# A gated recurrent layer on one Trainium2 core: its input products computed by a seven-product matrix algorithm nested twice, over 16 steps at a time

## The chip, the cores and the metric

The kernel runs on one core of one Trainium2 chip. The metric is the device time of one execution in microseconds. The profile is that of one execution, taken by the hardware profiler; PE is TensorE's matmuls, PEld its weight loads, DVE is VectorE, ACT ScalarE, POOL GpSimd, SP SyncE.

## The reference

B = 8 sequences, T = 512 steps, 512 inputs, 512 hidden units, all float32.

```python
def step(h, x_t):
    fused = jax.nn.sigmoid(jnp.concatenate([x_t, h], axis=-1) @ w_W + w_b)
    hidden_state, output_state = jnp.split(fused, 2, axis=-1)
    memory_state = x_t @ wx_W + wx_b + hidden_state * (h @ wh_W + wh_b)
    h_new = output_state * h + (1.0 - output_state) * jnp.tanh(memory_state)
    return (h_new, h_new)
_, hs = jax.lax.scan(step, h0, xT)
x = x + jnp.swapaxes(hs, 0, 1)
```

The products with x_t do not depend on h and can be computed steps ahead (the x side). The products with h are the recurrence: each step needs the one before.

## The kernel before, in words

**Layout.** The 512 units are four chunks k of 128 partitions. A matmul has a stationary operand of 128 x 32 (for h: 32 columns, in which the 8 sequences of a step have their place; for x: 4 steps x 8 sequences) and writes 32 of the 128 PSUM partitions; j = 0 to 3 selects which. Four matmuls with j = 0 to 3 run side by side in the array (a quad). A float32 matmul is issued as two instructions (passes). hT holds the state, in two halves: hTA (chunks 0 and 1) and hTB (chunks 2 and 3), in rings of NH = 8 steps.

**One step i** (line 370). TensorE first runs the recurrent matmuls in the order of ORDER: A0 A1 (256 columns, from hTA), A2 A3 (192, from hTB), D0 to D3 (128), H2 H3 (64), all accumulating on a bank that already holds the x side's part. Behind them `take(later, 1)` (line 397) issues one portion of x-side matmuls, up to the next `yield` in `products`. TensorE runs in this program order, so the x portion of step i lies between H of step i and A of step i + 1. On VectorE and ScalarE follows the chain of the step: `turn_r` transposes A's result (tr, line 415), ScalarE takes the sigmoid (md0A, line 226), VectorE scans (m, line 403), ScalarE takes tanh, and `update(0, q)` scans the new hTA (line 403), on which A0 and A1 of the next step wait. The same for the second half ends in `update(1, q)`, hTB, on which A2 and A3 wait. Behind these scans VectorE has the x-side work of the step, and two fillers (line 593); the next thing on it is tr of the next step. GpSimd adds x to the new state (ot, lines 594 to 600 and 615), behind hTB. The transpose of line 430 waits for the add of seven steps earlier.

**The x side.** Four steps are a group g; chunks c of 16 steps (four groups) are loaded by SP (`load_x`, three chunks ahead) and stored by SP (`store`). Groups 0 to 3 are computed plainly (`prefill`, 16 matmuls of 384 columns, four per yield). From there on, a block o of 8 steps (two groups) goes through `products` (line 296): the product of a 2 x 2 block matrix of x (2 groups of steps by 2 halves of the inputs) with a 2 x 2 block matrix of wx (2 halves of the inputs by 2 halves of the outputs) by seven block products instead of eight. The block sums of wx (tw) are made once on VectorE (`weight_sum`), those of x (sx) on GpSimd (`x_sum`), and the sums of the products are partly accumulated in the PSUM tiles xps and partly made by VectorE and ScalarE when these are read (lines 530 to 584). The results are in xs, one tile of 576 columns for each of two groups. ScalarE's `spread` (line 256) copies xs of the next group into the banks A, D and H, and `turn_x` (line 262) transposes its part X into md1 on VectorE, one piece a step.

What orders all this is the program order on each engine; the schedule is written by hand (lines 523 to 591: o is the block, u the step within it).

Of the kernel before, what the change touches and what calls it, by code (L numbers as in the profile page):

```python
# [13 lines left out]
P = 128  # L14
NQ = 4
# [19 lines left out]
WIDE = 384  # L35

SUMS = ((2,), (2,), (2, 1), (2, 1), (1,), (1, 3), (3,), (3, 3))

Q01, Q23 = slice(0, 64), slice(64, 128)
# [9 lines left out]
def tile_cond_rnn_residual(  # L49
# [100 lines left out]
    hT = [[pair(n, f"hT{n}{i}", 32, 3) for i in range(NH)] for n in "AB"]  # L150
# [22 lines left out]

    tw = [const.tile([P, 2, 2, WIDE], F32, name=f"tw{n}") for n in range(4)]
    sx = [[const.tile([P, 2, GS * B], F32, name=f"sx{n}{q}") for q in range(2)] for n in range(4)]
    step_bias = const.tile([P, HALF], F32, name="stepbias")
    xs = [const.tile([P, 576], F32, name=f"xs{n}") for n in range(2)]
    u2 = const.tile([P, WIDE], F32, name="u2")
    u3 = const.tile([P, WIDE], F32, name="u3")
    both = const.tile([P, WIDE], F32, name="both")  # L180

# [28 lines left out]
    nc.vector.tensor_copy(bias, xps[0])  # L210
    for t_ in xs:
        nc.gpsimd.memset(t_[:, :64], 0.0)
        nc.gpsimd.tensor_copy(t_[:, 64:128], bias[:, :64])
        nc.gpsimd.tensor_copy(t_[:, 512:], bias[:, 448:])
    for hf in range(2):
# [32 lines left out]
    def prefill_two():  # L248
        yield from prefill(2)
        yield from prefill(3)  # L250

    def source(g, c0, c1):

        return xs[g % 2][:, c0:c1] if g else xps[0][:, c0 - 64 : c1 - 64]
# [12 lines left out]
    def wx_of(kh, nh):  # L267
        return wx[:, 2 * kh : 2 * kh + 2, 2 * nh : 2 * nh + 2]

    def x_half(o, n, kh):  # L270

        return x_of(o // 2, slice(2 * kh, 2 * kh + 2), 8 * (o % 2) + GS * n, GS)

    def weight_sum(n, k=slice(0, 2), j=slice(0, 2)):

        a, b = [
            (wx_of(0, 1), wx_of(0, 0)),
            (wx_of(1, 1), tw[0]),
            (wx_of(1, 1), wx_of(0, 1)),
            (wx_of(1, 0), tw[1]),  # L280
        ][n]
        at = (slice(0, P), k, j)
        nc.vector.tensor_tensor(tw[n][at], a[at], b[at], ALU.subtract)  # L283

    def x_sum(o, n):

        t_ = [q[o % 2] for q in sx]
        a, b, op = [
            (x_half(o, 1, 0), x_half(o, 1, 1), ALU.add),
            (t_[0], x_half(o, 0, 0), ALU.subtract),  # L290
            (x_half(o, 0, 0), x_half(o, 1, 0), ALU.subtract),
            (x_half(o, 0, 1), t_[1], ALU.subtract),
        ][n]
        nc.gpsimd.tensor_tensor(t_[n], a, b, op)

    def products(o):

        t_ = [q[o % 2] for q in sx]
        p1 = (0, x_half(o, 0, 0), wx_of(0, 0))
        p2 = (0, x_half(o, 0, 1), wx_of(1, 0))  # L300
        p3 = (0, t_[3], wx_of(1, 1))
        p4 = (1, x_half(o, 1, 1), tw[3])
        p6 = (0, t_[1], tw[1])
        p7 = (1, t_[2], tw[2])

        def pair(left, right, k, c0=0, c1=WIDE):
            for j in range(NQ):
                bank, lhs, rhs = left if j < 2 else right
                mm(
                    xps[bank][32 * j : 32 * j + 32, COLS.start + c0 : COLS.start + c1],  # L310
                    lhs[:, k],
                    rhs[:, k, j % 2, c0:c1],
                    start=right is p7 and k == 0 and c0 == 0 and j >= 2,
                )

        def shared(k):
            for j in range(NQ):
                c0 = HALF * (1 - j // 2)
                mm(
                    xps[j // 2][32 * j : 32 * j + 32, COLS.start : COLS.start + HALF],  # L320
                    t_[0][:, k],
                    tw[0][:, k, j % 2, c0 : c0 + HALF],
                )

        pair(p1, p7, 0, 0, 128)
        if o > 2:
            yield
        pair(p1, p7, 0, 128)
        pair(p1, p7, 1, 0, 56)
        yield  # L330
        pair(p1, p7, 1, 56)
        yield
        pair(p2, p6, 0)
        yield
        pair(p2, p6, 1)
        yield
        pair(p4, p3, 0, 0, 344)
        yield
        pair(p4, p3, 0, 344)
        shared(0)  # L340
        pair(p4, p3, 1, 0, 72)
        yield
        shared(1)
        pair(p4, p3, 1, 72, 208)
        yield
        pair(p4, p3, 1, 208)
# [7 lines left out]
    def x_side():  # L354
        for o in range(2, NG // 2):
            yield from products(o)
# [5 lines left out]
    first = {1: prefill(1), 2: prefill_two()}  # L362
    weight_sum(0)
    spread(0, "HDA")
    for e in range(NQ):
        turn_x(0, e)

    pool_done = {}
    summed = []
    for i in range(T):  # L370
# [23 lines left out]
        if 1 <= i < 4:  # L394
            take(first[2], 2 if i == 3 else 3)
        else:
            take(later if i else first[1], 1)

        rows = slice(B * s, B * s + B)

# [84 lines left out]
        def update(hf, q):  # L485
            s1 = (i + 1) % GS
# [36 lines left out]
        o, u = divmod(i, 2 * GS)  # L523
        nxt, two = o + 1 < NG // 2, o + 2 < NG // 2
        if i == 0:
            nc.scalar.copy(xs[1][:, SC], xps[1][:, COLS])
            spread(1, "H")
            turn_x(1, 0)
        add_ = nc.vector.tensor_tensor
        if u == 3 and o and nxt:  # L530
            add_(xs[0][Q23, SC], xps[0][Q23, COLS], both[Q23], ALU.add)
        elif u == 7 and two:
            nc.vector.tensor_copy(xs[0][Q01, SC], xps[0][Q01, COLS])
        elif u == 0 and o and nxt:
            add_(u3[Q23], xps[1][Q23, COLS], u2[Q23], ALU.add)
        ahead = 2 * o + (1 if u < 3 else 2 if u < 7 else 3)
        if ahead < NG:
            turn_x(ahead, (u + 1) % GS)
        lo = slice(COLS.start, COLS.start + HALF)
        if u == 0:  # L540
            spread(2 * o + 1, "D")
            if o and nxt:
                nc.scalar.copy(xps[0][Q01, lo], step_bias[Q01])
                nc.scalar.copy(xps[1][Q23, lo], step_bias[Q23])
        elif u == 1:
            spread(2 * o + 1, "A")
            if o == 0:
                seed(3)
        elif u == 2:
            if o == 0:  # L550
                nc.scalar.copy(xs[0][:, SC], xps[0][:, COLS])
            elif nxt:
                nc.scalar.copy(both[Q23, HALF:], xps[0][Q01, lo])
                nc.vector.tensor_copy(both[Q23, :HALF], xps[1][Q23, lo])
            if two:
                nc.scalar.copy(xps[0][Q01, COLS], bias[Q01, COLS])
                if o:
                    x_sum(o + 2, 2)
        elif u == 3:
            if o == 0:  # L560
                nc.scalar.copy(xs[1][:, SC], xps[1][:, COLS])
                x_sum(o + 2, 2)
        elif u == 4 and nxt:
            if o:
                add_(xs[1][Q01, SC], xps[1][Q01, COLS], u3[Q23], ALU.add)
            spread(2 * o + 2, "A")
            if two:
                x_sum(o + 2, 0)
        elif u == 5 and nxt:
            if o:  # L570
                add_(xs[1][Q23, SC], u3[Q23], both[Q23], ALU.add)
            if two:
                nc.scalar.copy(xps[0][Q23, COLS], xps[0][Q01, COLS])
                x_sum(o + 2, 1)
            spread(2 * o + 2, "D")
        elif u == 6 and nxt:
            spread(2 * o + 2, "H")
            if two:
                nc.vector.memset(xps[1][Q01, COLS], 0.0)
                x_sum(o + 2, 3)  # L580
        elif u == 7 and nxt:
            if two:
                nc.scalar.copy(u2[Q23], xps[0][Q23, COLS])
            spread(2 * o + 3, "H")
        if i < len(SUMS):
            for n in SUMS[i]:
                weight_sum(n, *divmod(summed.count(n), 2))
                summed.append(n)
        if i == 4:
            for to, c_ in ((Q01, slice(256, 448)), (Q23, slice(64, 256))):  # L590
                nc.vector.tensor_tensor(step_bias[to], bias[Q23, c_], bias[Q01, c_], ALU.subtract)
# [22 lines left out]
        for hf in (1, 0):  # L614
# [79 lines left out]
```

## Time and profile before

| | |
|---|---|
| median of 3 runs | 1654.95 us (1654.7 to 1655.07) |
| the profiled execution | 1654.78 us, its span 1653.0 us |
| A start of step 1 | 20.10 us |
| A starts of steps 4, 14, 494 and 511 | 33.09, 65.65, 1592.34, 1645.85 us |
| granted TensorE clock, steps 14 to 493 | 1.00 |
| DVE busy, steps 14 to 493 | 1341.98 us, 2.80 a step |

An "A start" is the start of the first matmul A<-wa,hTA of a step; from one to the next is one step. In the timeline a row has its start, its length, engine, line, operation, tiles, shapes and the count of merged instructions, and in brackets the idle time before it with what ended it. Matmul ends are modelled and overlap the next matmuls, so TensorE's pace is read from starts.

### The profile page before, as it was taken

What the parts mean: (1) busy time and instruction counts of PE and PEld (TensorE: products, weight loads), DVE (VectorE), ACT (ScalarE), POOL (GpSimd) and SP (SyncE); (2) the same over time, 40 slices, a digit from 0 to 9 for tenths busy, and PEclk for the clock granted to TensorE, in tenths of its full rate; (3) what the DMA queues carried; (4) which work ended last, traced back from release to release, by engine and by line L of the source; (5) the groups of instructions that cost most, each with busy time, mean ns of one, the idle gap of its engine ahead of it and who ended that gap; (6) DMA issues with size and microseconds to landing.
All of it is one profiled execution on the core that took longest, in us unless ns stands there. A gap on an engine that the chain in (4) does not pass through costs nothing.

```text
span 1653.0 us, 114239 instructions
## 1 busy us (share of the span) xinstructions
PE 1640.8 (99%) x47566; PEld 1291.2 (78%) x47566; DVE 1438.5 (87%) x11237; ACT 1136.4 (69%) x5884; POOL 328.7 (20%) x1290
## 2 busy tenths in 40 slices
PE   8999999999999999999999999999999999999998
PEld 5777778777777777777877777777777777787776
DVE  6888888888888888888888888888888888888887
ACT  4667767667677676676776766767767667677665
POOL 2221121211211212112112121121121211211211
PEclk9999999999999999999999999999999999999999
DMA  4000000000000000000000000000000000000000
GB/s 181 17 5 17 17 17 17 16 5 17 17 17 17 5 17 17 17 17 4 17 17 17 17 15 7 17 18 17 17 4 18 17 17 17 4 17 11 11 11 10
DMA packets 11473, 30.41 MB, mean 18 GB/s; under 512 B 1221, under 2 KB 1733, under 8 KB 10953
## 3 DMA queue, kind: packets, MB, share of 16 engines
q1 hardware_dynamic: 10800, 22.94, 4.0%
q8 instruction: 372, 6.09, 1.5%
q14 instruction: 149, 1.21, 0.2%
q10 hardware_dynamic: 152, 0.16, 0.0%
HBM read 14.70 MB, written 8.39 MB: 14 GB/s over the span
## 4 chain that ended last, share of the span: by engine, by line
PE 97%; DVE 2%; DMA 1%; issue 0%; ACT 0%; DVEq 0%
PE A L195 47%; PE D L195 26%; PE xp L195 17%; PE H L195 7%; DMA wd<-in_wd_dram 1%; DVE m L403 0%; DVE tr L415 0%; DMA rows<-in_bias_dram 0%; DVE md1B L472 0%; DVE tw L283 0%; DVE md1A L430 0%; DVE hTA L403 0%; DVE tz L415 0%; DVE hTB L403 0%; DVE md1B L430 0%
## 5 line engine op out<-in xcount | busy, mean ns | idle before, releaser
L195 PE MATMUL A<-wa,hTA 128*32 128x256 f32 x8176 | 535.4, 379 | 2.8 <-DVE hTA L403 2.7
L195 PE MATMUL A<-wa,hTB 128*32 128x192 f32 x8176 | 427.8, 327 | 0.0
L195 PEld LDWEIGHTS A<-wa,hTA 128*32 128x32 f32 x8176 | 271.2, 122 | 167.5 <-DVE hTA L403 81.4
L595 POOL TENSOR_TENSOR ot<-xin,hTB 128x16 f32<-128x16 f32 x503 | 125.4, 249 | 1284.3 <-DVE hTB L403 1273.6
L195 PEld LDWEIGHTS A<-wa,hTB 128*32 128x32 f32 x8176 | 255.4, 123 | 133.3 <-DVE hTB L403 101.6
L195 PE MATMUL D<-wd,hTA 128*32 128x128 f32 x8192 | 317.6, 273 | 1.2 <-DMA wd<-in_wd_dram 1.2
L195 PE MATMUL D<-wd,hTB 128*32 128x128 f32 x8192 | 317.6, 273 | 0.0
L226 ACT ACTIVATE md0A<-tr 128x16 f32<-128x16 f32 x512 | 112.8, 220 | 239.4 <-DVE tr L415 224.9
L195 PE MATMUL xp<-tw,sx 128*32 128x192 f32 (+5 forms) x2480 | 276.3, 358 | 0.0
L195 PEld LDWEIGHTS D<-wd,hTA 128*32 128x32 f32 x8192 | 257.0, 122 | 22.5 <-DMA wd<-in_wd_dram 1.5
L415 DVE STREAM_TRANSPOSE tr<-A 128x64 f32<-128x64 f32 x511 | 127.7, 250 | 145.6 <-PE A L195 137.8
L195 PEld LDWEIGHTS D<-wd,hTB 128*32 128x32 f32 x8192 | 240.4, 122 | 0.1
L226 ACT ACTIVATE hTB<-m 128x8 f32<-128x8 f32 x1024 | 163.6, 208 | 90.0 <-DVE m L403 85.0
L195 PE MATMUL xp<-wx,xin 128*32 128x384 f32 (+4 forms) x1552 | 218.9, 384 | 0.0
L195 PE MATMUL H<-wa,hTB 128*32 128x64 f32 x8192 | 208.2, 219 | 0.0
L195 PEld LDWEIGHTS H<-wa,hTB 128*32 128x32 f32 x8192 | 185.6, 122 | 0.0
L226 ACT ACTIVATE hTB<-hTB 128x16 f32<-128x16 f32 x512 | 121.2, 237 | 85.0 <-DVE hTB L403 84.2
L403 DVE TENSOR_TENSOR_SCAN hTA<-hd0A,hTA 128x24 f32<-128x24 f32 x1024 | 175.9, 172 | 0.0
L403 DVE TENSOR_TENSOR_SCAN hTB<-hd0B,hTB 128x24 f32<-128x24 f32 x1024 | 154.4, 192 | 21.8
L226 ACT ACTIVATE hTA<-m 128x8 f32<-128x8 f32 x1024 | 160.7, 206 | 2.3
L403 DVE TENSOR_TENSOR_SCAN m<-md0B,md1B 128x24 f32<-128x24 f32 x1024 | 154.6, 192 | 1.3
L403 DVE TENSOR_TENSOR_SCAN m<-md0A,md1A 128x16 f32<-128x16 f32 x1024 | 141.9, 180 | 8.9
(104 smaller groups left out, 2717.1 us busy)
## 6 DMA issues: line engine op xcount, KB each, us to landing
xin<-in_x_dram SPq DMA_DIRECT2D x31, 256.0 KB, 3.2
out_dram<-ot SPq DMA_DIRECT2D x31, 256.0 KB, 2.1
wx<-in_wx_dram SPq DMA_DIRECT2D x4, 768.0 KB, 7.0
wa<-in_wa_dram SPq DMA_DIRECT2D x4, 512.0 KB, 9.7
wd<-in_wd_dram SPq DMA_DIRECT2D x1, 768.0 KB
wd<-in_wd_dram SPq DMA_DIRECT2D x1, 256.0 KB, 11.2
out_dram<-ot SPq DMA_DIRECT2D x1, 192.0 KB, 3.8
head<-in_xh_dram ACTq DMA_DIRECT2D x1, 144.0 KB, 5.0
```

The lines of the kernel that those rows point to most:

```text
L195: nc.tensor.matmul(out_, lhsT, rhs, start=start, stop=False, skip_group_check=True)
L226: inst = nc.scalar.activation(out_, in_, func, **kw).ins
L403: return nc.vector.tensor_tensor_scan(*[t_[:, :, c_].rearrange("p n c s -> p (n c s)") for t_ in (out_, d0, d1)], 0.0, ALU.mult, ALU.add,).ins
L415: inst = nc.vector.transpose(t_.rearrange("p c n -> p (c n)"), raw[n][hf]).ins
L595: return engine.tensor_tensor(ot[:, t, 2 * hf : 2 * hf + 2, :].rearrange("p c n -> p n c"), x_of(c, slice(2 * hf, 2 * hf + 2), t, 1).rearr ...
```

## The change

The seven-product algorithm is applied to blocks of 16 steps, and each of its seven products is again computed by seven products. The outer level splits x into 2 pairs of groups and 2 halves of the inputs, and the 384 output columns of each quarter into 2 halves of 192; the inner level splits each pair into its groups, each half of the inputs into its two chunks, and the 192 columns into 2 of 96. That makes 49 products for a chunk, each with one chunk of 128 inputs, 32 rows and 96 columns for each j.

- `products(c)` goes through seven stages (one for each inner product q, in the order 2 5 3 1 6 7 4). A stage has seven products, one for each outer product p: three in PSUM tile xps[0] and four in xps[1], at 96 columns each. Every product is one yield; a step takes three, every sixteenth step four.
- When the last product of a stage in one of the two PSUM tiles is issued, the same step gets a `drain` on VectorE: one tensor_tensor of 288 or 384 columns, PSUM plus an SBUF tile (a bias, or an earlier drain), into ee or ff. 14 drains in 16 steps.
- `result` makes the outer sums on GpSimd: two times seven additions of 192 columns a chunk, at most two a step, into xs, which now has four tiles (one for each group of a chunk).
- The sums of x are 4 outer (128 columns) and 12 inner ones (32 to 128 columns) a chunk on GpSimd, two a step in eight steps. The inner sums of the weights (ti, 24 sums of 384 or 768 columns) are made once on GpSimd, four ahead of step 0 and the rest in steps 0 to 12. The outer sums (tw) stay on VectorE, three whole ones ahead of step 0 and the fourth in quarters in steps 0 to 3.
- Chunk 1 (groups 4 to 7) is computed plainly like chunk 0, in steps 4 to 13. The products of chunk c are issued from step 16c - 18 on, those of the last chunk end at step 493.
- GpSimd's two adds a step (L595) become one of 32 columns, ahead of the step's sums on GpSimd; for that hTA and hTB lie in one tile.
- The ScalarE and VectorE copies of lines 530 to 584 go. `spread` is at the first three steps of a group (A, D, H), after the drain and turn_x.

```diff
+BL = 96
+STAGES = (2, 5, 3, 1, 6, 7, 4)
+FRESH = (2, 5, 1)
+SLOTS = ((1, 6, 7), (2, 3, 4, 5))
+LEAD = 18
+PLAIN = (2, 3, 5, 6, 8, 10, 11, 13, 14, 16)
...
+    def products(c):
+        for q in STAGES:
+            for bank in range(2):
+                for n, p in enumerate(SLOTS[bank]):
+                    for j in range(NQ):
+                        mm(
+                            xps[bank][32 * j : 32 * j + 32, BL * n : BL * n + BL],
+                            left(c, p, q),
+                            right(p, q, j),
+                            start=q in FRESH and n == 0,
+                        )
+                    yield
+
+    def drain(q, bank):
+        at, n = (slice(0, 3), 3) if bank == 0 else (slice(3, 7), 4)
+        to, with_ = {
+            2: (ee[0], off[0]),
+            5: (ee[1], off[1]),
+            3: (ee[2], off[1]),
+            1: (ff[0][:, :, 0], ee[0]),
+            6: (ff[0][:, :, 1], ee[2]),
+            7: (ff[1][:, :, 1], ee[1]),
+            4: (ff[1][:, :, 0], off[0]),
+        }[q]
+        src = xps[bank][:, : BL * n].rearrange("p (n b) -> p n b", n=n)
+        nc.vector.tensor_tensor(to[:, at], src, with_[:, at], ALU.add)
+
+    def result(e, n):
...
+        to, a, b = [
+            (f[1], f[0], f[1]),
+            (f[2], f[1], f[2]),
+            (y[0][0], f[3], f[0]),
+            (f[4], f[4], f[6]),
+            (y[0][1], f[4], f[1]),
+            (y[1][0], f[5], f[2]),
+            (y[1][1], f[6], f[2]),
+        ][n]
+        nc.gpsimd.tensor_tensor(to, a, b, ALU.add)
...
     weight_sum(0)
+    weight_sum(2)
     spread(0, "HDA")
     for e in range(NQ):
         turn_x(0, e)
+    weight_sum(1)
+    for n in (0, 2):
+        for p in (0, 2):
+            inner_weight(n, p)
...
+    for c in range(2, NCH):
+        w0 = TC * c - LEAD
+        for n, q in enumerate(x_sums(c)):
+            at_step(w0 - (13 if c > 2 else 10) + n // 2, q)
+        done = 0
+        for w in range(TC):
+            n = done
+            done += 3 + w // 15
+            for m, q in enumerate(STAGES):
+                for bank in range(2):
+                    if n < 7 * m + 3 + 4 * bank <= done:
+                        drains.setdefault(w0 + w, []).append((q, bank))
+        for e, w in ((0, 11), (1, 15)):
+            for n in range(7):
+                at_step(w0 + w + n // 2, (result, e, n))
...
+        elif i < 4 + len(PLAIN):
+            take(first[4], PLAIN[i - 4] - (PLAIN[i - 5] if i > 4 else 0))
         else:
-            take(later if i else first[1], 1)
+            take(later, 4 if (i + LEAD) % TC == TC - 1 else 3)
...
+        for d in drains.get(i, ()):
+            drain(*d)
+        ahead = (i + 5) // GS
...
+        elif ahead < NG:
+            turn_x(ahead, (i + 1) % GS)
+            if s < 3:
+                spread(ahead, "ADH"[s])
...
-        for hf in (1, 0):
-            pool_done[i + 1] = add(hf, nc.gpsimd)
+        pool_done[i + 1] = nc.gpsimd.tensor_tensor(
+            ot[:, t],
+            x_of(c, slice(0, NQ), t, 1),
+            hTs[(i + 1) % NH][:, :, :, B * s1 : B * s1 + B, 2].rearrange("p h c n -> p (h c) n"),
+            ALU.add,
+        ).ins
+        for job, *args in jobs.get(i, ()):
+            job(*args)
```

More of the change, by code (lines that the diff above doesn't have):

```diff
@@ L246, in prefill, with prefill_all @@
             yield
-    def prefill_two():
-        yield from prefill(2)
-        yield from prefill(3)
+    def prefill_all(*groups):
+        for g in groups:
+            yield from prefill(g)
     def source(g, c0, c1):
-        return xs[g % 2][:, c0:c1] if g else xps[0][:, c0 - 64 : c1 - 64]
+        return xs[g % GS][:, c0:c1] if g else xps[0][:, c0 - 64 : c1 - 64]
     def spread(g, names):
@@ L288, in x_sum, with x_block @@
+    def x_block(c, r, kh):
+        return xins[c][:, :, 2 * kh : 2 * kh + 2, 32 * r : 32 * r + 32]
+    def x_sum(c, n):
+        t_ = so[c % 2]
         a, b, op = [
[L289 to L292, printed above, removed]
-        ][n]
[L294 to L346, printed above, removed]
@@ L354, in x_side @@
     def x_side():
-        for o in range(2, NG // 2):
-            yield from products(o)
+        for c in range(2, NCH):
+            yield from products(c)
     seed(1)
@@ L361, in tile_cond_rnn_residual @@
     later = x_side()
-    first = {1: prefill(1), 2: prefill_two()}
+    first = {1: prefill(1), 2: prefill_all(2, 3), 4: prefill_all(4, 5, 6, 7)}
     weight_sum(0)
+    weight_sum(2)
     spread(0, "HDA")
@@ L536, in tile_cond_rnn_residual @@
[L536 to L591, printed above, removed]
+        for d in drains.get(i, ()):
+            drain(*d)
+        ahead = (i + 5) // GS
+        if i < 3:
+            spread(1, "HDA"[i])
+            turn_x(1, i)
+            if i == 2:
+                turn_x(1, 3)
+        elif ahead < NG:
+            turn_x(ahead, (i + 1) % GS)
+            if s < 3:
+                spread(ahead, "ADH"[s])
```

138 lines of the change are left out of this document (105 added, 33 removed).

## The prediction, made before the changed kernel was run

> **What bounds the kernel now.** I read the page first, then the matmuls in order of time in the middle of the run and at its end, then VectorE and GpSimd in the same steps, then the groups by form.
>
> ```profile
> span 1653.0 us, 114239 instructions
> PE 1640.8 (99%) x47566; PEld 1291.2 (78%) x47566; DVE 1438.5 (87%) x11237; ACT 1136.4 (69%) x5884; POOL 328.7 (20%) x1290
> PE 97%; DVE 2%; DMA 1%; issue 0%; ACT 0%; DVEq 0%
> ```
>
> By the page TensorE alone sets the time, and 12.5% less x work would simply come off. But this is a recurrence, so the question is how long a step takes when TensorE has no x work. The run has such steps: the x products run ahead and are used up twelve steps before the end. Here are two A starts there, and the last one:
>
> ```profile
> 1627.08 1.09 PE L195 MATMUL A<-wa,hTA 128*32 128x256 f32 x16 [0.24 <-DVE hTA L403]
> 1628.00 0.87 PE L195 MATMUL A<-wa,hTB 128*32 128x192 f32 x16
> ...
> 1630.21 1.09 PE L195 MATMUL A<-wa,hTA 128*32 128x256 f32 x16 [0.24 <-DVE hTA L403]
> ...
> 1645.85 1.09 PE L195 MATMUL A<-wa,hTA 128*32 128x256 f32 x16 [0.24 <-DVE hTA L403]
> ```
>
> Six steps from 1627.08 to 1645.85 take 18.77, that is **3.128 us a step with no x work at all**. TensorE waits there, 0.24 us before A for hTA. This is the loop through VectorE and ScalarE: A's result, transposes, sigmoid, scan, tanh, scan, back into A. The middle of the run, between the A start of step 14 and that of step 494 (both ends are A starts), next to the tail and steps 4 to 13:
>
> ```profile
> 65.65:1592.34 1526.69, 1526.69 (x44645) 1209.01 (x44645) 1341.98 (x10502) 1066.71 (x5521) 301.98 (x1200) 1.00 0.05 14
> 1592.34:1645.85 53.51, 50.80 (x1436) 39.26 (x1432) 43.33 (x363) 33.78 (x186) 8.62 (x35) 1.00 0.04 13
> 33.09:65.65 32.56, 32.51 (x940) 25.09 (x936) 29.67 (x220) 21.37 (x111) 10.17 (x26) 1.00 0.02 4
> ```
>
> The first two numbers of a row are the length and TensorE's busy time, at a granted clock of 1.00. 480 steps in 1526.69 are 3.181 us each, with TensorE never idle. So two bounds lie 0.053 us apart: TensorE's stream at 3.181 and the recurrence at 3.128. Only the first of them is touched by fewer x columns.
>
> **What the x work costs TensorE, before and after.**
>
> ```profile
> 20.10 1.04 PE L195 MATMUL A<-wa,hTA 128*32 128x256 f32 x16
> ...
> 22.48 0.41 PE L195 MATMUL H<-wa,hTB 128*32 128x64 f32 x16
> 22.71 2.12 PE L195 MATMUL xp<-wx,xin 128*32 128x384 f32 x24
> 24.64 1.04 PE L195 MATMUL A<-wa,hTA 128*32 128x256 f32 x16
> ...
> 31.80 1.47 PE L195 MATMUL xp<-wx,xin 128*32 128x384 f32 x16
> 33.09 1.04 PE L195 MATMUL A<-wa,hTA 128*32 128x256 f32 x16
> ...
> 35.70 0.28 PE L195 MATMUL xp<-wx,xin 128*32 128x128 f32 x2
> ...
> 35.91 0.39 PE L195 MATMUL xp<-wx,xin 128*32 128x256 f32 x2
> ```
>
> Starts count, not the modelled durations. The recurrent matmuls take 22.71 - 20.10 = 2.61. Eight instructions of 384 columns (one yield of prefill: four matmuls in two passes) take a third of 24.64 - 22.71, 0.643. Four instructions run side by side as one quad: two quads of 128 columns take 35.91 - 35.70 = 0.21, so 0.105 to 0.109 each, and four quads of 64 (H) 0.23, so 0.056. A quad of 96 lies halfway, 0.0825, and one product of the change (four matmuls, two passes, so two quads) costs 0.165. That the 64-column quads keep the same rate per column shows that smaller matmuls with as many weight loads are no trap here.
>
> Columns: before, products(o) streams 2688 columns in 8 steps, 336 a step. After, 49 products of 96 are 4704 in 16 steps, 294. By TensorE alone a step with three products would take 2.61 + 3 x 0.165 = 3.108, and the one in 16 with four 3.273.
>
> **The sum.** (1) Steps 14 to 493, where the new products run (30 chunks of 16). Fifteen steps of 16 fall below the recurrence, so they take its time. I take 3.138: the tail's 3.128 and 0.010 for waits that the middle has and the tail has not, by one transpose in the tail (0.24) against its mean over all steps (0.258), rounded down as some of these waits hide:
>
> ```profile
> 1645.72 0.24 DVE L430 STREAM_TRANSPOSE md1B<-H 128x64 f32<-128x64 f32 x1
> ```
> ```profile
> L430 DVE STREAM_TRANSPOSE md1B<-H 128x64 f32<-128x64 f32 x512 | 132.0, 258 | 0.1
> L531 DVE TENSOR_TENSOR xs<-xp,both 64x384 f32<-64x384 f32 x62 | 34.8, 561 | 2.0
> L571 DVE TENSOR_TENSOR xs<-u,both 64x384 f32<-64x384 f32 x62 | 37.4, 603 | 0.8
> L554 DVE COPY both<-xp 64x192 f32<-64x192 f32 x62 | 22.4, 361 | 1.9
> L294 POOL TENSOR_TENSOR sx<-xin 128x64 f32<-128x64 f32 x124 | 40.2, 324 | 0.0
> ```
>
> 15 x 3.138 + 3.273 = 50.34 a chunk, x 30 = 1510.3, against 1526.7: **-16.4**. TensorE's own saving there would be 1526.7 - 30 x (15 x 3.108 + 3.273) = 29.9; the rest turns into TensorE waiting for hTA and hTB.
> (2) The tail, 17 steps: the x work ends at step 493 instead of some six steps later, 53.51 to 17 x 3.128 = 53.18: **-0.3**.
> (3) Chunk 1 becomes plain. PLAIN spreads 16 yields over steps 4 to 13, six steps with two (2.61 + 1.29 = 3.90, the 1.29 being 31.80 to 33.09) and four with one (3.26): 36.4 against 32.56: **+3.9**.
> (4) Start: two more whole weight sums on VectorE ahead of step 0, and 24 inner sums queued on GpSimd through step 12. Steps 1 to 3 last 3.9 to 4.5 us, which covers most of what these do to the scans; the four one-yield steps have a cover of only 0.13. Bounds 0 and 3; I take **+0.7**.
> Sum -12.1. The profiled execution took 1654.78 with its span of 1653.0; the median is 1654.95, 0.17 apart. So 1642.7.
>
> **VectorE in the steady steps.** Seven sums or copies in 8 steps go (L531 to L579), 14 drains in 16 steps come: never two in a step, none in two of them. Seven read 4 x 96 = 384 columns from PSUM, like L531 (bounds 0.55 to 0.60, L571 reading SBUF twice; I take 0.56), seven 288, between L554's 0.361 and 0.561, I take 0.46. VectorE's total hardly moves. What counts is whether a drain ends before the transpose that opens the next chain:
>
> ```profile
> 873.50 1.05 PE L195 MATMUL A<-wa,hTA 128*32 128x256 f32 x16
> 874.37 0.84 PE L195 MATMUL A<-wa,hTB 128*32 128x192 f32 x16
> ```
> ```profile
> 874.07 0.30 DVE L403 TENSOR_TENSOR_SCAN hTB<-hd0B,hTB 128x24 f32<-128x24 f32 x2
> 874.41 0.56 DVE L531 TENSOR_TENSOR xs<-xp,both 64x384 f32<-64x384 f32 x1
> 875.00 0.21 DVE L265 STREAM_TRANSPOSE md1A<-xs 128x32 f32<-128x32 f32 x1
> 875.17 0.07 DVE L593 MEMSET idle<- 128x1 f32 x2
> 875.27 0.25 DVE L415 STREAM_TRANSPOSE tr<-A 128x64 f32<-128x64 f32 x1
> ...
> 875.80 0.28 DVE L403 TENSOR_TENSOR_SCAN m<-md0A,md1A 128x16 f32<-128x16 f32 x2
> ```
>
> This is the order that the change makes in 14 of 16 steps: hTB, a 384-wide sum, turn_x, the fillers, tr. From the end of hTB (874.37) to tr 0.90 us pass, and everything fits with 0.03 to spare; the fillers end at 875.24. So a 0.56 drain is free, and behind it wait turn_x, the fillers and tr, on which ScalarE's sigmoid hangs. The drain itself waits for the step's x products, which are done before A starts. The next stage's first product in that bank waits for the drain, a whole step later. ScalarE loses all its PSUM copies and keeps only spread.
>
> **GpSimd in the steady steps.** The two adds of L595 become one, and every step gets one or two more sums: x sums of 32 to 128 columns in eight steps, results of 192 columns in the other eight (two in six of them, one in two). Readers of the results (turn_x, spread) come a step or more later; the store and load queue on SP waits only for the add, which stays first. These sums read SBUF, and so do the scans.
>
> ```profile
> 880.81 0.61 DVE L571 TENSOR_TENSOR xs<-u,both 64x384 f32<-64x384 f32 x1
> ```
> ```profile
> 874.45 0.25 POOL L595 TENSOR_TENSOR ot<-xin,hTB 128x16 f32<-128x16 f32 x1 [2.72 <-DVE hTB L403]
> 874.65 0.25 POOL L595 TENSOR_TENSOR ot<-xin,hTA 128x16 f32<-128x16 f32 x1
> 874.86 0.32 POOL L294 TENSOR_TENSOR sx<-xin 128x64 f32<-128x64 f32 x1
> ...
> 880.75 0.25 POOL L595 TENSOR_TENSOR ot<-xin,hTB 128x16 f32<-128x16 f32 x1 [2.44 <-DVE hTB L403]
> 880.96 0.57 POOL L595 TENSOR_TENSOR ot<-xin,hTA 128x16 f32<-128x16 f32 x1
> ```
>
> The second add of the lower step takes 0.57 instead of 0.25 and ends 0.11 after a VectorE sum of two SBUF inputs (880.81 + 0.61): the two exclude each other. The Trainium skill ("SBUF — State Buffer", Who interferes with whom) states this rule, that a VectorE instruction with two SBUF inputs and a GpSimd instruction that reads SBUF block each other whole; the trace agrees (0.57 against 0.25). A drain has one input in PSUM; a scan has two in SBUF. So GpSimd must be done before the first m scan, 2.30 after A (875.80 - 873.50). The add starts 0.95 after A (874.45 - 873.50), the first result some 0.24 later at 1.19, and two results of length d end at 1.19 + 2d - 0.045, since neighbours overlap by some 45 ns (874.65 + 0.25 against 874.86). From 16 columns (0.25) to 64 (0.324) the slope is 1.55 ns a column, so 192 columns make d = 0.52 and the end 2.18: free, hidden beside the drain and the transposes. It costs from d = 0.58 on, or from 0.63 if the reads are over 0.11 ahead of the recorded end, as that last 0.11 suggests.
>
> **Rivals.** *The stream gives the time* (the tail's wait is not the bound with x work in between): 1642.7 - (29.9 - 16.4) = 1629.2. Against it: in the tail nothing but the loop holds the step. For it: there 0.92 lie between A's hTA part and its hTB part, in the middle 0.87, so some of the tail's 3.128 may be weight loads that x work would have let through earlier.
> *Drains or waits a little longer*: a 384 drain at 0.60 delays tr by 0.04 in 7 of 16 steps, 210 x 0.04 = +8.4; with waits of the L430 kind doubled, +4.8: about 1653.
> *Slower, GpSimd's results hold the m scan*: with d = 0.70 two results end at 2.545, and the scan starts 0.14 to 0.25 late in 6 of 16 steps, which goes straight into a loop without slack: 180 x 0.19 = +34, 1677. It exceeds the kernel before once the scan is 0.07 late (180 x 0.067 = 12.1), d about 0.64. For it: the slope rests on two small sizes; against: it would have to be 1.6 times as steep.
> By the Trainium skill ("GPSIMD Engine Reference", Elementwise — side-by-side cycle accounting) a sum of two inputs costs about 2.6 cycles an element at 1.2 GHz; an estimate from that is d = 0.63 and 2.41 for the end, so up to 0.11 late in 180 steps, +0 to +19 and 1643 to 1662. The trace's slope of 1.55 speaks against it, but only up to 64 columns.
>
> **How the numbers follow.** Forecast (1634 to 1649) 0.50; the stream 0.12; longer drains or waits (1649 to 1659) 0.18; GpSimd 0.20. 0.2%, about what this measurement can tell from no change, is 3.3 us: faster is below 1651.6. Faster 0.50 + 0.12 + 0.05 = 0.67, same 0.11, slower 0.22. The range 1629 to 1668 leaves 0.06 below and 0.12 above.
>
> **What would show it.** Right: A starts 3.13 to 3.14 apart with x work, "idle before" at A or at its weight loads put down to hTA or hTB, TensorE's busy share down to some 98%, 3.27 once in 16 steps, tr about 1.77 after A, the last GpSimd sum ended before the m scan, and a start of steps 4 to 13 of 36 to 37 us. Wrong: steps of 3.11 (the stream), tr later than 1.80 after A (drains), m scans late behind a GpSimd sum, or quads of 96 further apart than 0.085.

## The result and the profile after

The changed kernel takes **1646.18 us** (median of 4, 1645.51 to 1646.84); the kernel before took 1654.9 beside it (4 runs, 1654.7 to 1655.07). The ratio is 0.9947, 95% interval 0.993 to 0.9965. The gain is 8.7 us, the forecast was 12.1 (1642.7).

The profiled execution of the changed kernel took 1646.05 with a span of 1644.0. From its page the lines that answer to those of before, and from the lists of groups the weight loads of A, of the changed kernel (L203) and of the kernel before (L195):

```profile
PE 1628.2 (99%) x53006; PEld 1360.1 (83%) x53006; DVE 1379.4 (84%) x11215; ACT 976.8 (59%) x5520; POOL 569.3 (35%) x1467
...
PE 97%; DVE 2%; POOL 1%; DMA 0%; issue 0%; ACT 0%; DVEq 0%; POOLq 0%
...
L203 PEld LDWEIGHTS A<-wa,hT 128*32 128x32 f32 x16352 | 507.7, 123 | 241.4 <-DVE hT L511 138.9
```
```profile
L195 PEld LDWEIGHTS A<-wa,hTA 128*32 128x32 f32 x8176 | 271.2, 122 | 167.5 <-DVE hTA L403 81.4 <-issue 0.7 <-DVE idle L468 0.2
L195 PEld LDWEIGHTS A<-wa,hTB 128*32 128x32 f32 x8176 | 255.4, 123 | 133.3 <-DVE hTB L403 101.6
```

By the first lines nothing has changed in kind: TensorE busy 99%, the chain 97% on it. The weight loads of A stood idle for 241.4 us, 138.9 of these until VectorE's scan had written hT. That does not tell the loop from the stream either: before, they stood idle for 167.5 + 133.3 = 300.8 us, 183.0 of these for the scans. So the bound has to be read from the steps themselves, and from runs with less work.

The stretches between A starts (the first two numbers are length and TensorE's busy time): steps 1 to 3, 4 to 13, 14 to 493, the tail.

```profile
20.69:35.41 14.72, 13.72 (x304) 8.48 (x308) 13.19 (x69) 7.01 (x36) 11.80 (x13) 1.00 0.02 6
35.41:72.50 37.09, 37.06 (x933) 26.13 (x929) 26.29 (x219) 22.74 (x118) 20.39 (x38) 1.00 0.01 4
72.50:1583.92 1511.42, 1510.97 (x50164) 1278.78 (x50160) 1281.95 (x10495) 908.83 (x5158) 512.76 (x1357) 1.00 0.05 15
1583.92:1637.00 53.08, 48.99 (x1373) 37.66 (x1361) 39.10 (x354) 31.52 (x180) 8.38 (x24) 1.00 0.04 12
```

| term | forecast | measured |
|---|---|---|
| steps 14 to 493 | -16.4 | 1511.42 - 1526.69 = -15.3 |
| tail | -0.3 | 53.08 - 53.51 = -0.4 |
| chunk 1 plain, with the delays of steps 4 to 13 | +3.9 | 37.09 - 32.56 = +4.5 |
| start, up to the A of step 4 | +0.7 | 35.41 - 33.09 = +2.3 |
| sum | -12.1 | -8.9 |

Two steps in the middle, and TensorE around the one step in 16 with four products:

```profile
427.87 1.73 PE L203 MATMUL A<-wa,hT 128*32 128x256 f32 x32
...
430.29 0.41 PE L203 MATMUL H<-wa,hT 128*32 128x64 f32 x16
430.51 0.35 PE L203 MATMUL xp<-wx,xin 128*32 128x96 f32 x8
430.68 0.35 PE L203 MATMUL xp<-wx,so 128*32 128x96 f32 x8
430.84 0.35 PE L203 MATMUL xp<-tw,xin 128*32 128x96 f32 x8
431.01 1.72 PE L203 MATMUL A<-wa,hT 128*32 128x256 f32 x32
```
```profile
875.35 1.73 PE L203 MATMUL A<-wa,hT 128*32 128x256 f32 x32
...
878.64 1.70 PE L203 MATMUL A<-wa,hT 128*32 128x256 f32 x32
...
881.75 1.05 PE L203 MATMUL A<-wa,hT 128*32 128x256 f32 x16
```

431.01 - 427.87 is 3.14 a step. Products follow each other by 0.17 and 0.16 (0.165 was worked out), and H starts 2.42 after A. The wait for hT lies inside A: 2.64 pass from A to the first product, where TensorE needs 2.61 (from the trace of before); three products of 0.165 bring that to 3.135, and the next A follows at once. The step with four products takes 3.29, the one after it 3.11, which is TensorE's own time for three products (2.61 + 3 x 0.165 = 3.105) with no wait in it. Over all chunks the medians are 3.300 and 3.105, and 3.131 to 3.136 in the other 14 positions, whether a drain lies in the step or not.

VectorE and GpSimd in the same step, one with a 288-wide drain and two results:

```profile
428.59 0.18 DVE L511 TENSOR_TENSOR_SCAN hT<-hd0B,hT 128x24 f32<-128x24 f32 x1
428.69 0.43 DVE L403 TENSOR_TENSOR ee<-xp,off 128x288 f32<-128x288 f32 x1
...
429.67 0.25 DVE L523 STREAM_TRANSPOSE tr<-A 128x64 f32<-128x64 f32 x1 [0.40 <-PE A L203]
...
430.20 0.28 DVE L511 TENSOR_TENSOR_SCAN m<-md0A,md1A 128x16 f32<-128x16 f32 x2
```
```profile
428.85 0.26 POOL L675 TENSOR_TENSOR ot<-xin,hT 128x32 f32<-128x32 f32 x1 [1.78 <-DVE hT L511]
429.07 0.60 POOL L418 TENSOR_TENSOR xs<-ff 128x192 f32<-128x192 f32 x1
429.62 0.60 POOL L418 TENSOR_TENSOR ff<-ff 128x192 f32<-128x192 f32 x1
```

tr starts 1.80 after A and has waited 0.40 for TensorE's A, not for the drain. The second result ends at 430.22, the scan starts at 430.20 and takes its usual 0.28. So everything fits, on GpSimd with nothing to spare.

At the start it does not fit. GpSimd, then VectorE:

```profile
15.95 5.58 POOL L315 TENSOR_TENSOR ti<-wx 128x768 f32<-128x768 f32 x4
...
22.63 3.15 POOL L315 TENSOR_TENSOR ti<-wx,ti 128x768 f32<-128x768 f32 x2
```
```profile
17.71 1.10 DVE L511 TENSOR_TENSOR_SCAN m<-md0A,md1A 128x16 f32<-128x16 f32 x2
...
19.43 1.20 DVE L511 TENSOR_TENSOR_SCAN hT<-hd0A,hT 128x24 f32<-128x24 f32 x1
...
23.13 1.77 DVE L296 TENSOR_TENSOR tw<-wx,tw 128x384 f32<-128x384 f32 x1
24.84 0.24 DVE L523 STREAM_TRANSPOSE tr<-A 128x64 f32<-128x64 f32 x1
```

Every one of these has two inputs in SBUF. Scans of 0.17 and 0.28 take 1.2 and 1.1, and a weight sum takes 1.77, holding up the tr behind it. Step 1 lasts 6.19 in place of 4.54.

### The profile page after: what moved, and what is told of

Same layout as the page of the kernel before. It is cut to its first block, busy times and chain, and to the rows that moved or that the text cites. A ratio compares the mean times of both kernels' runs of the same rounds, so it can differ in the third digit from the quotient of the medians.

```text
span 1644.0 us, 124813 instructions
## 1 busy us (share of the span) xinstructions
PE 1628.2 (99%) x53006; PEld 1360.1 (83%) x53006; DVE 1379.4 (84%) x11215; ACT 976.8 (59%) x5520; POOL 569.3 (35%) x1467
## 3 DMA queue, kind: packets, MB, share of 16 engines
q8 instruction: 414, 6.78, 1.7%
## 4 chain that ended last, share of the span: by engine, by line
PE 97%; DVE 2%; POOL 1%; DMA 0%; issue 0%; ACT 0%; DVEq 0%; POOLq 0%
PE A L203 48%; PE D L203 26%; PE xp L203 16%; PE H L203 7%; DVE tr L523 0%; DVE m L511 0%; POOL ti L315 0%; DMA rows<-in_bias_dram 0%; DVE hT L511 0%; POOL xs L225 0%; DVE md1B L580 0%; DVE md1A L538 0%; DVE tz L523 0%; POOL off L229 0%; DVE tw L296 0%
## 5 line engine op out<-in xcount | busy, mean ns | idle before, releaser
L203 PE MATMUL A<-wa,hT 128*32 128x256 f32 x16352 | 885.9, 356 | 5.7 <-DVE hT L511 5.2
L203 PEld LDWEIGHTS A<-wa,hT 128*32 128x32 f32 x16352 | 507.7, 123 | 241.4 <-DVE hT L511 138.9
L203 PE MATMUL D<-wd,hT 128*32 128x128 f32 x16384 | 543.1, 273 | 1.0 <-DMA wd<-in_wd_dram 1.0
L203 PEld LDWEIGHTS D<-wd,hT 128*32 128x32 f32 x16384 | 482.8, 122 | 21.7 <-DMA wd<-in_wd_dram 1.3
L243 ACT ACTIVATE hT<-m 128x8 f32<-128x8 f32 x2048 | 324.4, 207 | 98.0 <-DVE m L511 97.7
L243 ACT ACTIVATE hT<-hT 128x16 f32<-128x16 f32 x1024 | 233.1, 228 | 85.0 <-DVE hT L511 84.2
L203 PE MATMUL H<-wa,hT 128*32 128x64 f32 x8208 | 210.3, 219 | 0.0
L203 PEld LDWEIGHTS H<-wa,hT 128*32 128x32 f32 x8208 | 187.5, 122 | 0.0
L511 DVE TENSOR_TENSOR_SCAN hT<-hd0A,hT 128x24 f32<-128x24 f32 x1024 | 176.3, 172 | 0.0
L511 DVE TENSOR_TENSOR_SCAN hT<-hd0B,hT 128x24 f32<-128x24 f32 x1024 | 154.4, 192 | 21.8
L203 PE MATMUL xp<-ti,si 128*32 128x96 f32 x5040 | 150.1, 246 | 0.2 <-issue 0.2
```

The lines of the kernel that those rows point to most:

```text
L203: nc.tensor.matmul(out_, lhsT, rhs, start=start, stop=False, skip_group_check=True)
L243: inst = nc.scalar.activation(out_, in_, func, **kw).ins
L511: return nc.vector.tensor_tensor_scan(*[t_[:, :, c_].rearrange("p n c s -> p (n c s)") for t_ in (out_, d0, d1)], 0.0, ALU.mult, ALU.add,).ins
```

## The experiments

Theory going in: with 294 columns a step the loop through VectorE and ScalarE sets steps 14 to 493; drains and results are free; what the forecast missed is the start. Rivals: TensorE's stream still sets the steps; GpSimd or the drains have their share. Ratios are to the kernel before, run on the same chip, with 95% intervals; its medians beside the three groups of runs were 1654.90, 1655.02 and 1655.12.

**less_x: is it the loop?** Two of every seven products of a stage are left out.

```diff
                 for n, p in enumerate(SLOTS[bank]):
+                    if n == 2 + bank:
+                        yield
+                        continue
```

> Two of the seven products of each stage are left out (one of three in the first PSUM tile, one of four in the second), so the output lacks part of the x side; everything else stays, drains and sums too. Theory 1, the loop through VectorE and ScalarE sets a step: a step stays at 3.13 us, only the step with four products falls from 3.30 to 3.13, and the time to about 1642 (30 x 0.14 less than 1646). Rival, TensorE's stream sets it: 5/7 of 0.495 is 0.354, steps of 2.97, and 1646 - 480 x 0.14 = about 1578.

Measured 1637.41 (1636.86 to 1637.55), 0.9892 (0.9879 to 0.9906).

```profile
72.91:1575.59 1502.68, 1502.68 (x46804) 1204.28 (x46800) 1280.18 (x10493) 908.55 (x5158) 512.74 (x1357) 1.00 0.05 15
```

With two sevenths of the x work gone, steps 14 to 493 lose 8.7 of 1511.4 us and still take 3.131 each; the stream would have lost some 67. The loop is the bound. TensorE's busy time equals the stretch here, with that much work missing, so a full busy time says nothing about the bound. The 8.7 has three parts: the step with four products and the next (3.300 + 3.105 - 2 x 3.133 = 0.139, 30 times 4.2), late steps (below; some 3), and 3.131 against 3.133.

**third_sum: would a longer GpSimd job hold the scans?** One more sum of 192 columns behind each of three results in seven; nothing uses it.

```diff
...
         nc.gpsimd.tensor_tensor(to, a, b, ALU.add)
+        if n % 2:
+            nc.gpsimd.tensor_tensor(extra, f[3], f[6], ALU.add)
```

> A third sum of 192 columns, whose result nobody reads, is added on GpSimd behind the two in the six steps of 16 that have two. The trace of the changed kernel has one at 0.596 us, so the third would run from about 2.3 to 2.85 us after A, over the first two m scans (2.33 to 2.60). Theory, the two exclude each other: the scans of these steps come 0.2 to 0.4 us late and all of it shows, 180 x 0.3 = +54, so about 1700 (1680 to 1720). Rival, short scans pass beside a GpSimd sum: no change, 1646.

Measured 1709.34 (1709.3 to 1709.38), 1.0327 (1.0308 to 1.0346). TensorE, VectorE and GpSimd in one of its steps with three sums:

```profile
904.36 1.79 PE L204 MATMUL A<-wa,hT 128*32 128x256 f32 x32 [0.18 <-DVE hT L514]
907.92 0.44 PE L204 MATMUL A<-wa,hT 128*32 128x256 f32 x4 [0.18 <-DVE hT L514]
```
```profile
906.75 0.71 DVE L514 TENSOR_TENSOR_SCAN m<-md0A,md1A 128x16 f32<-128x16 f32 x2
```
```profile
905.62 1.15 POOL L419 TENSOR_TENSOR xs<-ff 128x192 f32<-128x192 f32 x2
906.74 0.59 POOL L421 TENSOR_TENSOR extra<-ff 128x192 f32<-128x192 f32 x1
```

The pair of m scans takes 0.71 in place of 0.28 and ends at 907.46, just behind the third sum (907.33), and the step takes 3.56 in place of 3.13. In four steps of 16 the whole 0.43 goes into the time, in two others 0.35 and 0.04: the run gets 63 us longer. That a late scan makes the step late by as much is a second witness for the loop. So the rival of the forecast was a real mechanism; two sums escape it, three do not.

**no_results: do the results cost anything as they stand?** Their additions are left out.

```diff
+    c_out = False
...
-        nc.gpsimd.tensor_tensor(to, a, b, ALU.add)
+        if c_out:
+            nc.gpsimd.tensor_tensor(to, a, b, ALU.add)
```

> The 14 sums of 192 columns a chunk on GpSimd are left out, so xs keeps old values and the output lacks the x side of later chunks. Theory, they end just ahead of the m scans and cost nothing: the time stays within 1 us of 1646. Rival, they already hold the scans: with 2 x 0.596 they end at 2.34, and if that delayed m by 0.02 to 0.05 in six steps of 16, the time would fall by 4 to 9 us.

Measured 1645.35 (1644.91 to 1646.62), 0.9941 (0.9928 to 0.9955), a range that overlaps that of the changed kernel. They cost nothing that shows.

**no_inner and start: the start.** no_inner leaves the inner weight sums out. start keeps all of them: those that the first products need are made by VectorE ahead of step 0 and in steps 0, 1 and 3, GpSimd gets the other 17, one a step, and the sum of weight quarters moves from steps 0 to 3 to steps 5, 7, 8 and 10.

```diff
     for n in (0, 2):
-        for p in (0, 2):
-            inner_weight(n, p)
+        inner_weight(n, 0, nc.vector)
...
+    on_vector = {0: [(0, 2), (0, 3)], 1: [(0, 4), (0, 5)], 3: [(2, 2)]}
+    on_pool = [(2, 3), (1, 2), (1, 0), (2, 4), (1, 3), (1, 4), (1, 5), (2, 5), (3, 2), (3, 3), (3, 4)]
+    on_pool += [(0, 6), (3, 0), (1, 6), (2, 6), (3, 6), (3, 5)]
+    for n, w in enumerate(on_pool):
+        at_step(n, (inner_weight, *w))
...
```

> The 24 inner weight sums on GpSimd are left out and ti is zero, so most of the x side from chunk 2 on is wrong. Theory, these sums of 1.0 to 1.6 us hold the scans of steps 0 to 4: the A start of step 1 returns from 20.7 to 20.1, that of step 4 from 35.4 to about 33.1, steps 4 to 13 from 37.1 to 36.5, and the time falls by 2.5 to 3, to about 1643.3. Rival, the two additional weight sums on VectorE delay the start: no change, 1646.

> The same computation with another order of the inner weight sums: two on VectorE ahead of step 0, five more on VectorE in steps 0, 1 and 3, the other 17 on GpSimd at one a step in steps 0 to 16, and the four quarters of the last outer sum on VectorE in steps 5, 7, 8 and 10. If sums on GpSimd that hold the scans are what the start costs: A start of step 1 at 20.1 to 20.3, of step 4 at 33.1 to 33.4, steps 4 to 13 at 36.5 to 36.8, and 2 to 3 us less, about 1643.5. If it is the amount of work ahead of step 0 on VectorE: the A start of step 1 stays at 20.7 or grows, and 1646 or more.

Measured: no_inner 1642.73 (1641.61 to 1643.9), 0.9926 (0.9914 to 0.9939); start 1642.78 (1641.17 to 1644.42), 0.9926 (0.9914 to 0.9939). VectorE and the first two stretches of start:

```profile
17.68 0.28 DVE L510 TENSOR_TENSOR_SCAN m<-md0A,md1A 128x16 f32<-128x16 f32 x2
```
```profile
20.06:33.05 12.99, 12.99 (x308) 8.81 (x304) 10.12 (x75) 7.58 (x40) 5.18 (x6) 1.00 0.03 10
33.05:69.47 36.42, 36.42 (x932) 26.70 (x928) 26.29 (x213) 22.01 (x113) 20.12 (x36) 1.00 0.02 4
```

The scans are back at 0.28, steps 1 to 3 at the 12.99 of the kernel before, steps 4 to 13 at 36.42, and step 14 starts 3.03 earlier than in the changed kernel. In no_inner step 14 starts at 69.40, in start at 69.47: in this order the sums are free. start is the fastest complete kernel of the study, 3.4 us below the changed one by the medians; the ranges of the times lie apart, the intervals of the two ratios overlap (0.9930 to 0.9939).

**even, start_even: spread the products evenly.** The 49 products are cut at multiples of 6 columns into 16 equal portions, 3 1/16 products a step, which was to recover the 0.139 of each chunk. start_even is the same on top of start.

```diff
+        for w in range(TC):
+            u0, u1 = 49 * w, 49 * w + 49
+            for v in range(u0 // TC, -(-u1 // TC)):
+                q, bank, n, p = todo[v]
+                c0, c1 = 6 * max(0, u0 - TC * v), 6 * min(TC, u1 - TC * v)
...
```

> The 49 products of a chunk are cut at multiples of 6 columns, so that each of the 16 steps takes 3 1/16 products in place of fifteen with 3 and one with 4. Loop theory: a step of 3 1/16 products needs 2.613 + 0.505 + some 0.01 for the cut quads = 3.13 of TensorE, about the loop; the pair of 3.300 and 3.105 becomes two of 3.133 to 3.14, 30 x 0.13 = 4 us less, about 1642 (1641 to 1645, as narrow quads may cost more than their columns). Stream theory: the same columns and more quads, no change or slower by 480 x 0.01, 1646 to 1651.

> Both edits together. They act in different parts of the run (steps 0 to 13, and 14 to 493), so they should add: about 1639.5, from 1646 less 2.5 less 4.

Measured 1693.67 (1690.49 to 1696.05), 1.0233 (1.0219 to 1.0247), and 1693.29 (1690.45 to 1699.51), 1.0239 (1.0222 to 1.0255): 48 us slower, and no theory had it. The largest unexplained wait of even, in its list of waits (us, times, longest), and its steps 14 to 493:

```profile
PEld xp L203 <- issue: 31.2, 101, 0.7
```
```profile
72.91:1633.77 1560.86, 1547.63 (x53765) 1382.51 (x53760) 1288.02 (x10493) 907.67 (x5158) 512.70 (x1357) 1.00 0.05 15
```

"issue" is time in which the engine waited for nothing that the profile shows. The columns are the same; the instructions are more: 53765 + 53760 matmuls and weight loads in 480 steps, 224 a step against (50164 + 50160) / 480 = 209. A new theory: TensorE's instructions arrive no faster than 256 in 1560.86 x 256 / 107525 = 3.72 us.

**halves: more instructions alone.** One product a step is cut in two halves of 48 columns, and the portions per step stay as in the changed kernel.

```diff
+                    cuts = (0, 48, BL) if done % 3 == 0 else (0, BL)
+                    done += 1
+                    for c0, c1 in zip(cuts, cuts[1:]):
...
```

> One product of every step is issued as two matmuls of 48 columns in place of one of 96: the same columns, 16 more TensorE instructions (matmuls and weight loads) a step, 225 in place of 209. Theory, TensorE's instructions do not come faster than about 256 in 3.7 us (the kernel cut at 6 columns, with 224 a step, ran at 256 in 3.72 us, showed waits marked issue, and lost 47 us): 225 take 3.26 us, so 0.11 x 480 = +53, about 1695 (1680 to 1705). Rival, the very narrow quads of 6 to 30 columns were what cost there: 48-column quads cost 0.005 a step, and 1646 to 1649.

Measured 1721.34 (1720.78 to 1724.11), 1.0402 (1.0388 to 1.0416).

```profile
PEld xp L203 <- issue: 41.2, 114, 0.8
```
```profile
72.47:1659.54 1587.07, 1557.88 (x54244) 1363.92 (x54240) 1291.37 (x10498) 908.33 (x5160) 512.42 (x1357) 1.00 0.05 15
```

The same two views: 226 instructions a step and 3.306 us a step; 3.72 per 256 would make 3.28. The expected 1680 to 1705 was too low: the run is 75 us longer than the changed kernel. Two halves of a product, then the two whole products of the step:

```profile
97.03 0.35 PE L203 MATMUL xp<-wx,xin 128*32 128x48 f32 x16
97.19 0.51 PE L203 MATMUL xp<-tw,so 128*32 128x96 f32 x16
```

The two halves take 0.16 (97.03 to 97.19), no more than the 0.165 of a whole product. So neither uneven cuts nor the time of the 48-column matmuls cost the 75 us; the number of instructions does.

**start_quarters: a cheaper cut.** Units of 24 columns, 12 or 13 of them a step, on top of start: 212 instructions a step.

```diff
+            u0, u1 = u1, u1 + 12 + w // 12
...
```

> The kernel with the new order of the weight sums (1642.8), and in place of fifteen steps of three products and one of four, twelve of three and four of three and a quarter: three cuts of 24 columns a chunk, 212 TensorE instructions a step. Loop theory: the pair of 3.300 and 3.105 becomes four steps of about 3.155 and the 3.105, 30 x 0.09 = 2.7 less, 1640. Instruction supply: 212 in 3.13 us are 256 in 3.78, nearer to the limit of about 3.7 than the 3.86 now, so part of the gain or all of it may go in waits marked issue: up to 1645.

Measured 1646.43 (1645.49 to 1649.7), 0.995 (0.9937 to 0.9962): 3.6 slower than start. Its mean step in the middle is 3.158 against 3.152.

| kernel | TensorE instructions a step | us per 256 of them | us a step |
|---|---|---|---|
| before | 186 | 4.38 | 3.181 |
| less_x | 195 | 4.11 | 3.131 |
| third_sum | 209 | 4.01 | 3.278 |
| after (the changed kernel) | 209 | 3.86 | 3.149 |
| start_quarters | 212 | 3.81 | 3.158 |
| even | 224 | 3.72 | 3.252 |
| halves | 226 | 3.75 | 3.306 |

**start_load, start_quarters_load: the late steps.** Some steps of the changed kernel are late by 0.4 to 0.65: 130, 145 and 370, each one or two steps into a chunk, where the next x is loaded. The edit puts that load at the middle of the chunk in the program.

```diff
-        if t == 0 and c > 0:
+        if t == TC // 2 and c > 0:
```

> The kernel with the new order of the weight sums (1642.8), its x loads moved from the first step of a chunk, where the store of the last chunk still runs, to the ninth. The late steps of these runs (0.1 to 0.8 us, marked issue) lie in the second to fifth step of a chunk. If the 512 KB of load and store together delay the fetch of TensorE's instructions, half of these delays or more go: some 2 us less, 1640 to 1641.5. Rival, they come from TensorE's own pace: no change, 1642 to 1643.5.

> Both of the last two edits on the kernel with the new order of the weight sums. If both work as said: 1642.8 - 2.7 - 2 = about 1638. If instruction supply takes the cuts back: about 1641 to 1643.

Measured 1643.29 (1641.66 to 1643.81), 0.9925 (0.9913 to 0.9938), and 1646.27 (1644.32 to 1649.22), 0.9941 (0.9927 to 0.9954): no change from start and start_quarters. But the load has not moved. In start_load it is still issued 0.44 behind the store of the last chunk, as in start (429.01 and 429.45):

```profile
429.17 0.34 SPq L668 DMA_DIRECT2D out_dram<-ot  x1
429.61 0.38 SPq L119 DMA_DIRECT2D xin<-in_x_dram  x1
```

Each load between chunks starts in the first step of a chunk in both runs, as before the edit: on SP the load is still the next thing behind that store, and nothing in the program makes it wait for the ninth step. So these runs repeat start and start_quarters, and whether load or store makes those steps late was not tested.

**Where the unexplained waits fall.** The traces settle what kind of wait this is. The weight loads at which the changed kernel is late in steps 130, 145 and 370, then the stretches between one such wait and the next, with the counts of matmuls and weight loads behind "x":

```profile
437.96 1.04 PEld L203 LDWEIGHTS A<-wa,hT 128*32 128x32 f32 x24 [0.55 <-issue]
```
```profile
488.58 0.12 PEld L203 LDWEIGHTS xp<-ti,si 128*32 128x32 f32 x3 [0.44 <-issue]
```
```profile
1193.56 1.09 PEld L203 LDWEIGHTS A<-wa,hT 128*32 128x32 f32 x24 [0.61 <-issue]
```
```profile
437.93:488.55 50.62, 50.40 (x1663) 42.64 (x1664) 42.49 (x350) 29.98 (x171) 17.40 (x46) 1.00 0.05 15
488.55:1193.53 704.98, 704.83 (x23417) 595.60 (x23417) 598.96 (x4905) 424.44 (x2411) 243.59 (x644) 1.00 0.05 15
```

And in halves the stretches between waits at 104.59 (a load for a product), 127.24 (for H) and 131.24 (for a product):

```profile
104.55:127.20 22.65, 22.40 (x768) 19.79 (x768) 18.59 (x149) 12.78 (x73) 8.23 (x20) 1.00 0.03 5
127.20:131.20 4.00, 3.57 (x128) 3.19 (x128) 3.21 (x28) 2.20 (x13) 1.37 (x3) 1.00 0.01 4
```

From wait to wait the instructions are whole multiples of 256: in halves 2 x 768 = 6 x 256 and 2 x 128 = 256. In the changed kernel TensorE also has a semaphore instruction in each chunk, which the counts behind "x" leave out, 1 in the first stretch and 14 in the second:

```profile
L203 PEldq EVENT_SEMAPHORE  x14: 51/51/51, 491.4 to 1145.2; - x14
```

With these, 1663 + 1664 + 1 = 13 x 256 and 2 x 23417 + 14 = 183 x 256. Counted this way, all waits of weight loads for "issue" that are longer than 0.2 us in steps 14 to 493, 96 in even and 139 in halves, lie at one of two neighbouring places in every 256. The operation at the wait differs (A, H, a product), the place does not; a limit on the pace of single instructions would favour no place. And the changed kernel's instruction queue makes one transfer for each 256 of TensorE's instructions, 2 x 53006 / 256 = 414.1:

```profile
q8 instruction: 414, 6.78, 1.7%
```

In even it makes 442 (2 x 56606 / 256 = 442.2), in halves 446 (446.0). So TensorE waits at one place in each block of 256 instructions, and each block comes in one transfer of 16 KB (6.78 MB / 414); that the place is the beginning of a block is inferred. The changed kernel works off a block in 3.86 us on average and waits for few; even and halves would need one every 3.58 us or less to keep the loop's 3.13 (256 / 224 x 3.13) and wait often. 3.72 is a mean and no floor for a single block: two steps of halves without such a wait (114.40 to 120.68, 452 instructions) take 6.28, 3.56 per 256. The Trainium skill ("Runtime: NRT & Kernel Launch", Instruction fetch mechanics) describes refills in 16 KiB blocks of 256 instructions: the counts agree. It also holds the fetch to be hidden; the 31 and 41 us of waits in even and halves speak against that here.

## Why the prediction was right, and where its size was off

The sign and the mechanism held: the 0.053 between stream and loop was the gain to be had, not the 12.5% of x columns. By its steps:

- **Loop in place of stream**: shown by less_x, and by the late scans of third_sum. 3.138 was forecast for a step, 3.131 to 3.136 came. "With TensorE never idle", from which the prediction took that the stream set the steps before, rests on the busy time, which less_x shows to be no witness; the columns do bear it out, as 2.61 + 336 / 96 x 0.165 = 3.19 against the 3.181 measured.
- **The step with four products**: 3.273 forecast, 3.300 measured, and a following step of 3.105, TensorE's own pace, that the forecast had not. The pair costs 0.139 a chunk, where the forecast has 3.273 - 3.138 = 0.135: right in sum.
- **Late steps**: some 3 us in the middle of the profiled execution, the largest of them at the one place in a block of instructions; not foreseen. The prediction looked at columns and weight loads ("no trap here"), not at the supply of instructions. That the middle came within 1.1 of the forecast (-15.3 against -16.4) is in part luck: steps 0.004 shorter than forecast, 420 of them, take back some 2.
- **Chunk 1 plain**: +3.9 forecast; with the inner sums out of the way (no_inner, start) 36.42 - 32.56 = +3.9. Right.
- **Start: the term that was mis-sized.** "Bounds 0 and 3; I take +0.7." It is +2.3 up to step 4 and 37.09 - 36.42 = +0.7 more in steps 4 to 13: 3.0 in all, the upper bound. "Steps 1 to 3 ... cover most of what these do to the scans" failed: the inner sums hold the scans of steps 0 and 1 and a VectorE weight sum ahead of tr, and these stand on the loop however long TensorE's x work is. no_inner and start show it: without these sums beside the scans the 3.0 are gone. The exclusion was in the prediction, for the results; it was not applied to the start. The trace of before had only short GpSimd sums, so the length of a weight sum there (1.0 for 384 columns) was missing.
- **Drains**: free, as forecast. 288 columns took 0.43 (0.46 forecast).
- **Results on GpSimd**: free (no_results), but by less than was thought. d is 0.596, not 0.52:

```profile
L418 POOL TENSOR_TENSOR xs<-ff 128x192 f32<-128x192 f32 x240 | 140.6, 596 | 0.2
...
L349 POOL TENSOR_TENSOR si<-xin 128x64 f32<-128x64 f32 x60 | 19.3, 321 | 0.0
```

The slope is 2.15 ns a column (64 to 192), where the forecast took 1.55 from 16 and 64 columns. The estimate from the Trainium skill ("GPSIMD Engine Reference", Elementwise — side-by-side cycle accounting), with 2.6 cycles an element, was nearer: 0.63. d lies between the two points from which the prediction let it cost, 0.58 and 0.63, and the second held: two sums end 0.02 behind the start of the scan and do not hold it, so the sum's reads seem to be over ahead of its recorded end.
- **The indicators that failed**: "TensorE's busy share down to some 98%" did not come (99%); less_x shows 100% in its middle with two sevenths of the products out. "Idle before" at the weight loads came, put down to hT, but had been longer before (300.8 against 241.4 us), so it could not have told right from wrong. The distance of A starts could, and did.

Open: why one block is late and the next is not in the changed kernel, with the load and the store at the start of a chunk as untested rivals, and what holds a block back: the transfers themselves take some 1.08 us each (1.7% of 16 x 1644.0 us, over 414), not 3.7. start could still lose its few late steps with fewer instructions; that was not tried.

## What to carry to other kernels

Fewer matmul columns pay only down to the next bound; read that bound from a stretch without the removed work, and check it by leaving out more of that work, since neither a busy share of 99% nor the waits of weight loads told the two bounds apart here. Keep long GpSimd sums out of every time in which VectorE scans or adds from two SBUF inputs on the critical loop, the first steps included; a reordering of the same sums was worth 3.4 us. Look into the trace whether an edit did what it was meant to do: the load that was moved in the program came at the same time as before. Count TensorE's instructions as well as its columns before matmuls are cut smaller, and where a wait is ended by nothing that the profile shows, count the instructions from one such wait to the next, semaphore instructions included.

## What the hardware showed that was not expected

- Matmuls and weight loads together ran at best at 256 in 3.72 us, 14.5 ns each, over 480 steps (even 3.72, halves 3.75), though single steps of halves ran at 3.56 and 32 of them (H) pass in 0.22 us in a burst, 7 ns each. From 209 a step to 226 the time rose by 75 us with the same columns, and the waits stand 256 instructions, or a multiple, apart, exactly, once semaphore instructions are counted.
- The step after a long one is shorter than the loop's usual 3.13: 3.105 behind 3.300, which is TensorE's own time for three products.
- A GpSimd sum holds a scan of VectorE as it holds an addition (0.28 to 0.71), and its last hundredths do not: scans at 430.20 ran unhindered beside a sum recorded to 430.22.
- Weight loads of A stood idle for the scans longer in the kernel before, where TensorE's stream set the middle steps (183.0 us), than in the changed kernel, where the loop did (138.9).
